# Two stacked graph layers by 2x2 block products: T and V one behind the other in all batches, M2 added by TensorE to a copy of M1 in PSUM, block products in another order

## The chip, the cores and the metric

The kernel runs on one core of a Trainium2 chip. The metric is the device time of one execution in microseconds (us), 2274.87 before (median of 3 runs, 2274.1 to 2276.31). The engines are named as in the profile: PE is TensorE (PEld its weight loads), DVE is VectorE, ACT is ScalarE, POOL is GpSimd, SP issues most DMAs.

## The reference

32 graphs of 512 nodes with 512 features; everything is float32. Two layers, each behind a layer norm and a ReLU, each added to its input:

```python
def _L0_gnn_ref(x, adj, W):
    deg = jnp.sum(adj, axis=-1, keepdims=True)
    agg = jnp.einsum('bij,bjf->bif', adj, x) / jnp.maximum(deg, EPS)
    cat = jnp.concatenate([x, agg], axis=2)
    return jax.nn.relu(jnp.einsum('bnf,of->bno', cat, W))

def _L1_gnn_ref(X, adj, mask, Wqk, Wv):
    q, k = jnp.split(X @ Wqk, 2, axis=-1)
    v = X @ Wv
    agg = jnp.einsum('bij,bjd->bid', adj, k * mask[:, :, None])
    w = inv_scale * mask * jnp.einsum('bid,bid->bi', q, agg)
    return jax.nn.softmax(w, axis=1)[:, :, None] * v

h = jnp.maximum(_layernorm(x, axis=-1), 0.0)
x = x + _L0_gnn_ref(h, adj, L0_gnn_W)
h = jnp.maximum(_layernorm(x, axis=-1), 0.0)
x = x + _L1_gnn_ref(h, adj, nodemask, L1_gnn_Wqk, L1_gnn_Wv)
```

## The kernel before, in words

**What is multiplied.** Per batch there are these products of 512x512 matrices. In layer 0: y = h W2 and o = h W1 + A y, with A the adjacency divided by the degrees. In layer 1, with h1 the normalised second input: u = A (masked h1), T = h1 (Wq Wk^T, scaled) and V = h1 Wv. Since q times the aggregated k is, row by row, the sum of T times u, the scores need only T and u. They are `dot` (T times u summed over a row), `scores`, a maximum over all nodes (`maximum`, on GpSimd), `exponents`, a sum (`row_sum`, on GpSimd) and `weights`. The output is the weights times V (`apply`) plus the layer's input, which a DMA adds (`add_x1`), and `store`.

**Seven block products in place of eight.** Each product is split into 2x2 blocks of 256. Seven products of block sums, M1 to M7, give the four blocks of the result:

- C11 = M1 + M2
- C12 = (M1 + M6) + (M5 + M3)
- C22 = (M1 + M6 + M7) + M5
- C21 = M1 + M6 + M7 + M4

The left operands are the four blocks and three sums of them (seven slots, `left_sums`), the right ones likewise (`right_sums`); the fourth sum overwrites a block. `LEFT` and `RIGHT` say which slot each M uses: M1 and M2 use blocks alone, M5 the first sums (slot 4), M6 the sums in slot 5, M7 those in slot 6. The function `product` does this for y, o and u. The bank `pp` in PSUM collects M1, then M6, M7 and M4 on top, and ScalarE copies the sum out between (`copy`). The bank `pr` holds M2, which VectorE adds to the copy of M1. The bank `pq` collects M5 and M3. One product M is 4 matmuls of 256 columns (8 in o, which has two terms).

**T and V** go one level deeper: each block product is again made of seven, so there are 49 products of 128x128 blocks for T and 49 for V, and the second level's sums (`recombine`, seven VectorE adds a matrix) are made afterwards from the tile `tv`. Both have the same left operand, `h1T`, so `layer1_tv` lays the right operands beside each other and computes T and V together: 49 matmuls of 256 columns, four banks to one M. The function `layer1_one` computes only one of the two, with 128 columns and two banks to one M; the kernel before uses it in its last turn (T and V of batch 30) and for T of batch 31, whose V is a plain `product`.

**Loop and order.** The order of instructions on each engine is written out by hand: `run` steps through a phase (a product M by M, or in half M's), and after each step's matmuls it emits what a `Plan` has at this step; then follows what the product itself does with its bank (a copy or an add). Per turn i of the main loop: o of batch i (14 steps), T and V of batch i-1 (14 steps), u of batch i (7 steps), y of batch i+1 (7 steps). The plans hang onto these steps: loading and normalising x of later batches and turning it by way of DRAM (`FrontH`, whose tile is `n` and whose result is `hT`), the same for the adjacency (`FrontA`: degree sums on ScalarE, `aT`), the second layer norm (`FrontH1`: statistics, `shift` which makes `nmr`, `write` which makes `h1m` and sends it out, `mask`), the block sums, and the tail of the batch before (`Post`). Batch 0 is prepared by `start` (its y and o are computed there), turns 1 and 2 have plans of their own because they also prepare batches 3 and 4, and the last turn has a plan of its own.

[...] The recombination of T is split in the plan: rows 0 in the last steps of T and V, rows 1 in u, each seven adds of 256 columns. The dots follow in u (steps 3 and 4), the scores at step 5, the softmax in y.

## Time and profile before

| What | Before |
|---|---|
| time, median of 3 | 2274.87 us |
| span of the profiled run | 2273.7 us |
| granted TensorE clock | 0.999 |
| DMA, mean over the span | 204 GB/s |
| matmul records on PE | 10526, of which 2940 in T and V together |
| steady period of one batch | 69.50 us |
| T and V in a period: PE, DVE, ACT busy | 21.15, 16.39, 15.03 us |
| last T and V to the end of the span | 68.1 us |

A record of a group has its line, engine, operation, output and inputs by the program's names, shape and count; then the busy time in us and the mean of one in ns; then the idle time just before, and what ended most of it. The names `ptv` and `pw` are the banks of `layer1_tv` and `layer1_one`; `pp_y`, `pq_u`, `pr_o` are those of `product`. Each float32 matmul of the program shows as two records.

### The profile page before, as it was taken

The numbers are of one execution on the slowest core, as the hardware profiler recorded it, in microseconds if no ns is written. First come the engines' busy times: TensorE is split into PE (matmuls) and PEld (weight loads), VectorE is DVE, ScalarE is ACT, GpSimd is POOL, SyncE is SP. The second block draws the span as 40 slices with busy tenths as digits, with TensorE's granted clock in tenths as the row PEclk, the third lists the DMA queues.
The fourth block names the chain that finished last, engine by engine and source line by source line (L and its number), as shares of the span: only waits on it lengthen the run. The fifth ranks groups of instructions, "written<-read, shape, count | busy, mean of one in ns | idle before, by whom it ended". The sixth has DMA issues, their size and how long they took to land.

```text
span 2273.7 us, 32878 instructions
## 1 busy us (share of the span) xinstructions
PE 2249.1 (99%) x10526; PEld 1975.5 (87%) x10526; DVE 1923.7 (85%) x3802; ACT 1026.9 (45%) x1896; POOL 173.2 (8%) x260
## 2 busy tenths in 40 slices
PE   7999999999999999999999999999999999999998
PEld 6788888888888888888888888888888888888897
DVE  6789888888888888888888888888888888888878
ACT  4454444445434554444454344544444543445323
POOL 0000000000010000100000000000000000000000
PEclk9999999999999999999999999999999999999999
DMA  9978787887878787877878778777888787888553
GB/s 220 235 212 244 207 207 190 211 232 204 208 200 202 215 223 203 208 190 209 233 204 207 200 199 218 223 204 208 187 211 230 206 206 200 202 217 218 149 129 90
DMA packets 409772, 463.68 MB, mean 204 GB/s; under 512 B 37728, under 2 KB 271712, under 8 KB 405376
## 3 DMA queue, kind: packets, MB, share of 16 engines
q1 hardware_dynamic: 400192, 428.56, 69.9%
q0 software_dynamic: 8928, 32.51, 8.6%
q8 instruction: 83, 1.36, 0.3%
q14 instruction: 89, 0.73, 0.1%
q10 hardware_dynamic: 480, 0.52, 0.1%
HBM read 293.93 MB, written 167.51 MB: 203 GB/s over the span
## 4 chain that ended last, share of the span: by engine, by line
PE 92%; DMA 3%; DVE 3%; SPq 1%; ACT 1%; issue 0%; POOL 0%; DVEq 0%; POOLq 0%; ACTq 0%
PE ptv L465 28%; PE pp_o L130 18%; PE pp_y L130 9%; PE pq_o L130 9%; PE pp_u L130 9%; PE pr_o L130 5%; PE pq_u L130 5%; PE pq_y L130 5%; PE pr_y L130 2%; PE pr_u L130 2%; PE pw L517 1%; DMA a<-in_adj_dram 1%; DVE tv L94 0%; DMA late<-in_nodemask_dram 0%; SPq L212 0%; DVE mv L97 0%
## 5 line engine op out<-in xcount | busy, mean ns | idle before, releaser
L465 PE MATMUL ptv<-mv,h1T 128*128 128x256 f32 x2940 | 639.7, 379 | 0.1
L465 PEld LDWEIGHTS ptv<-mv,h1T 128*128 128x128 f32 x2940 | 558.5, 190 | 76.4 <-DVE xu L444 0.5
L94 DVE TENSOR_TENSOR tv<-tv 128x256 f32<-128x256 f32 (+1 forms) x658 | 326.9, 509 | 13.5 <-ACT tv L100 1.5
L100 ACT ACTIVATE tv<-ptv 128x512 f32<-128x512 f32 (+1 forms) x360 | 184.9, 541 | 260.0 <-PE ptv L465 259.3
L130 PE MATMUL pp_y<-wide 128*128 128x256 f32 x1024 | 242.6, 380 | 0.9 <-ACT y L100 0.9
L130 PE MATMUL pp_o<-y,aT 128*128 128x256 f32 x1024 | 242.0, 379 | 0.0
L130 PE MATMUL pp_u<-h1m,aT 128*128 128x256 f32 x1024 | 242.0, 379 | 0.0
L130 PE MATMUL pp_o<-w,wide 128*128 128x256 f32 x992 | 234.3, 379 | 0.0
L130 PEld LDWEIGHTS pp_y<-wide 128*128 128x128 f32 x1024 | 194.9, 191 | 27.8 <-ACT y L100 1.3
L130 PEld LDWEIGHTS pp_u<-h1m,aT 128*128 128x128 f32 x1024 | 194.4, 190 | 27.0 <-issue 0.5
L130 PEld LDWEIGHTS pp_o<-y,aT 128*128 128x128 f32 x1024 | 194.4, 190 | 26.7 <-DVE y L97 0.3
L130 PEld LDWEIGHTS pp_o<-w,wide 128*128 128x128 f32 x992 | 188.5, 190 | 25.6
L100 ACT ACTIVATE o<-pp_o 128x512 f32<-128x512 f32 x96 | 57.3, 596 | 294.9 <-PE pp_o L130 294.9
L100 ACT ACTIVATE y<-pp_y 128x512 f32<-128x512 f32 x128 | 76.4, 597 | 235.9 <-PE pp_y L130 235.9
L94 DVE TENSOR_TENSOR tv<-ptv,tv 128x512 f32<-128x512 f32 x240 | 139.7, 614 | 42.9 <-PE ptv L465 39.4
L97 DVE TENSOR_TENSOR h1T<-h1T 128x512 f32<-128x512 f32 (+2 forms) x193 | 165.9, 873 | 1.2
L100 ACT ACTIVATE xu<-pp_u 128x512 f32<-128x512 f32 x128 | 76.4, 597 | 196.1 <-PE pp_u L130 196.1
L246 POOL TENSOR_TENSOR rstd<-rstd,mhalf 128x2 f32<-128x2 f32 (+1 forms) x96 | 78.9, 822 | 651.2 <-DVE rstd L245 651.2
L130 PE MATMUL pq_y<-wide 128*128 128x256 f32 x512 | 121.0, 379 | 0.0
L130 PE MATMUL pq_o<-y,aT 128*128 128x256 f32 x512 | 121.0, 379 | 0.0
L130 PE MATMUL pq_u<-h1m,aT 128*128 128x256 f32 x512 | 120.9, 379 | 0.0
L94 DVE TENSOR_TENSOR tv<-ptv,m_tv 128x512 f32<-128x512 f32 (+1 forms) x120 | 71.9, 622 | 56.4 <-PE ptv L465 54.5
(127 smaller groups left out, 3253.8 us busy)
## 6 DMA issues: line engine op xcount, KB each, us to landing
w<-dw SPq DMA_DIRECT2D x217, 256.0 KB, 4.1
xu<-in_x_dram SPq DMA_DIRECT2D x128, 256.0 KB, 5.4
a<-in_adj_dram SPq DMA_DIRECT2D x256, 128.0 KB, 3.1
dh1T<-h1m SPq DMA_DIRECT2D x128, 256.0 KB, 3.1
dx<-xu SPq DMA_DIRECT2D x32, 1024.0 KB, 4.9
sh1T<-dh1T SPq DMA_DIRECT2D x256, 128.0 KB, 3.2
shT<-dhT SPq DMA_DIRECT2D x248, 128.0 KB, 5.9
daT<-a SPq DMA_DIRECT2D x124, 256.0 KB, 3.0
```

The costliest lines, as they stand in the source:

```text
L94: (on or nc.vector).tensor_tensor(o, a, b, op=ALU.add)
L97: (on or nc.vector).tensor_tensor(o, a, b, op=ALU.subtract)
L100: nc.scalar.activation(o, i, AF.Copy)
L130: nc.tensor.matmul(p[:, rc, :], lt[:, LEFT[k], dk, ts(rc, P)], right[:, dk, :], start=first and n == 0, stop=True, skip_group_check=True,)
L246: nc.gpsimd.tensor_tensor(rstd[:, a:b], rstd[:, a:b], mhalf[:, a:b], op=ALU.pow)
L465: nc.tensor.matmul(banks[n][:, :, ts(i, P)], left[:, LEFT[k], LEFT_IN[j], :], mvR[:, RIGHT[k], RIGHT[j], :, :], start=first and i == 0, st ...
L517: nc.tensor.matmul(banks[n][:, ts(i, P)], held[:, s, :] if held is not None and j == 3 else left[:, s, LEFT_IN[j], :], mvR[:, RIGHT[k], RI ...
```

## The change

Three things. First, `layer1_tv` is gone: in all batches T and then V are computed by `layer1_one`, seven steps' worth of plan in each. This halves the number of banks that one M takes, and V's banks are written only after T's. Second, M2 is no longer put into a bank of its own and added by VectorE. ScalarE copies M1 from its bank into a bank of a new pool `ps_r` (two of the eight banks), and TensorE adds M2 to it there; what is read out is then C11 itself. In y, u, T and V ScalarE copies it out; in o VectorE reads it straight from PSUM. Batch 0's y and o keep the old way (`seed=False`). Third, the order of the block products is M1, M5, M6, M2, M7, M3, M4 in place of M1, M2, M6, M5, M7, M3, M4, so that M2 comes three products after M1. The plans follow: the recombination of T is done in V's steps 1 and 3 with whole rows, the dots and the scores move up in u, and the softmax from y into u.

```diff
-    ps_m = ctx.enter_context(tc.tile_pool(name="ps_m", bufs=8, space=bass.MemoryType.PSUM))
+    ps_m = ctx.enter_context(tc.tile_pool(name="ps_m", bufs=6, space=bass.MemoryType.PSUM))
+    ps_r = ctx.enter_context(tc.tile_pool(name="ps_r", bufs=2, space=bass.MemoryType.PSUM))
...
-    ORDER = [1, 2, 6, 5, 7, 3, 4]
+    ORDER = [1, 5, 6, 2, 7, 3, 4]
...
         pp = mm_tile(f"pp_{name}")
         yield from m(1, pp, True)
-        c11 = place(0, 0)
+        pr = seed_tile(f"pr_{name}")
+        c11 = pr if seed else place(0, 0)
         copy(c11, pp)
-        pr = mm_tile(f"pr_{name}")
-        yield from m(2, pr, True)
-        finish(0, 0, c11, pr, c11)
-        yield from m(6, pp, False)
-        c12 = place(0, 1)
-        copy(c12, pp)
         pq = mm_tile(f"pq_{name}")
         yield from m(5, pq, True)
         m5 = block(f"m5_{name}")
         copy(m5, pq)
+        yield from m(6, pp, False)
+        c12 = place(0, 1)
+        copy(c12, pp)
+        yield from m(2, pr, not seed)
+        if seed:
+            finish(0, 0, None, pr, None)
+        else:
+            finish(0, 0, c11, pr, c11)
         yield from m(7, pp, False)
...
-        yield from parts(1, pp, True, keep(0))
-        yield from parts(2, pr, True, plus(0))
+        yield from parts(1, pp, True, seed)
+        yield from parts(5, pq, True, keep5)
         yield from parts(6, pp, False, keep(1))
-        yield from parts(5, pq, True, keep5)
+        yield from parts(2, pr, False, keep(0))
         yield from parts(7, pp, False, lambda n, p: add(part(3, n), p, m5[n]))
...
-                if not last:
-                    for k in range(7):
-                        p.at(12 + k // 4, post.recombine, k, 0, 0)
-                    run(layer1_tv(i - 1), 14, p)
-                else:
-                    t_plan, v_plan = Plan(), Plan()
-                    for n, fs in p.items():
-                        (t_plan if n < 7 else v_plan)[2 * n % 14] = fs
-                    for k in range(7):
-                        v_plan.at(1 + 2 * (k // 4), post.recombine, k, None, 0)
+                t_plan, v_plan = Plan(), Plan()
+                for n, fs in p.items():
+                    (t_plan if n < 7 else v_plan)[2 * n % 14] = fs
+                for k in range(7):
+                    v_plan.at(1 + 2 * (k // 4), post.recombine, k, None, 0)
+                if last:
                     for c in range(C):
                         v_plan.at(5 + 2 * (c // 2), post.dot, c)
...
-                    run(layer1_one(i - 1, 0), 14, t_plan)
-                    run(layer1_one(i - 1, 1), 14, v_plan)
+                run(layer1_one(i - 1, 0), 14, t_plan)
+                run(layer1_one(i - 1, 1), 14, v_plan)
...
-                for k in range(7):
-                    p.at(1 + k // 4, post.recombine, k, 1, 0)
                 for c in range(C):
-                    p.at(3 + c // 2, post.dot, c)
-                p.at(5, post.scores)
-                p.at(5, post.maximum)
+                    p.at(1 + c // 2, post.dot, c)
+                p.at(2, post.scores)
+                p.at(2, post.maximum)
+                p.at(4, post.shift)
+                p.at(5, post.exponents)
+                p.at(6, post.row_sum)
...
                 if i > 0:
-                    p.at(0, post.shift)
-                    p.at(1, post.exponents)
-                    p.at(2, post.row_sum)
-                    p.at(4, post.weights)
+                    p.at(1, post.weights)
```

More of the change, by code (lines that the diff above doesn't have):

```diff
@@ L91, in mm_tile, with seed_tile @@
         return ps_m.tile([P, 2, H], F32, tag="m", name=name)
+    def seed_tile(name):
+        return ps_r.tile([P, 2, H], F32, tag="r", name=name)
     def add(o, a, b, on=None):
@@ L116, in of, with product @@
         return lambda i: t[:, i]
-    def product(name, terms, place, finish):
+    def product(name, terms, place, finish, seed=True):
         def m(k, p, first):
@@ L432, in layer0_y @@
         y = Y[b] = slots("yh", 1, f"y_{b}")
-        return product(f"y_{b}", [(hT, right(w2R))], *into(y))
+        return product(f"y_{b}", [(hT, right(w2R))], *into(y), seed=b > 0)
     def layer0_out(b, w1):
@@ L444, in finish @@
             nc.vector.scalar_tensor_tensor(dst, p, 0.0, dst, op0=ALU.max, op1=ALU.add)
-        return product(f"o_{b}", [(hT, w1), (AT_[b], right(Y[b]))], place, finish)
+        return product(f"o_{b}", [(hT, w1), (AT_[b], right(Y[b]))], place, finish, seed=b > 0)
     def layer1_u(b):
         return product(f"u_{b}", [(AT_[b], right(H1M[b]))], *into(U[b]))
-    def layer1_tv(b):
-        t = TV[b] = tv
-        left = H1T[b]
-        def m(k, banks, first):
-            for half in ((2, 1), (3, 0)):
-                for n in half:
-                    if first:
-                        banks[n] = mm_tile(f"ptv_{b}_{k}_{n}")
-                    for i, p in enumerate(range(2 * n, min(2 * n + 2, 7))):
-                        j = AT[p]
-                        nc.tensor.matmul(
-                            banks[n][:, :, ts(i, P)],
-                            left[:, LEFT[k], LEFT_IN[j], :],
-                            mvR[:, RIGHT[k], RIGHT[j], :, :],
-                            start=first and i == 0,
-                            stop=True,
-                            skip_group_check=True,
-                        )
-                yield half
-        def part(o, n):
-            first = [0, 4, 8, 10][n] + (2 if n < 2 else 3) * (o % 2)
-            return t[:, o // 2, :, first:first + min(2, 7 - 2 * n), :].rearrange("p w b f -> p w (b f)")
-        def parts(k, banks, first, use):
-            for half in m(k, banks, first):
-                yield
-                for n in half:
-                    use(n, banks[n][:, :, 0:P * min(2, 7 - 2 * n)])
-        def keep(o):
-            return lambda n, p: copy(part(o, n), p)
-        def plus(o):
-            return lambda n, p: add(part(o, n), p, part(o, n))
-        pp, pr, pq, m5 = {}, {}, {}, {}
-        def keep5(n, p):
-            m5[n] = block(f"m5_tv_{b}_{n}")[:, :, 0:P * min(2, 7 - 2 * n)]
-            copy(m5[n], p)
-        yield from parts(1, pp, True, keep(0))
-        yield from parts(2, pr, True, plus(0))
-        yield from parts(6, pp, False, keep(1))
-        yield from parts(5, pq, True, keep5)
-        yield from parts(7, pp, False, lambda n, p: add(part(3, n), p, m5[n]))
-        yield from parts(3, pq, False, plus(1))
-        yield from parts(4, pp, False, keep(2))
     def layer1_one(b, which, held=None):
@@ L549, in layer1_one, with seed @@
         pp, pr, pq, m5 = {}, {}, {}, {}
+        def seed(n, p):
+            pr[n] = seed_tile(f"pr_{which}_{b}_{n}").rearrange("p a f -> p (a f)")
+            copy(like(n, pr[n]), p)
         def keep5(n, p):
@@ L553, in keep5 @@
             copy(m5[n], p)
-        yield from parts(1, pp, True, keep(0))
-        yield from parts(2, pr, True, plus(0))
+        yield from parts(1, pp, True, seed)
+        yield from parts(5, pq, True, keep5)
         yield from parts(6, pp, False, keep(1))
-        yield from parts(5, pq, True, keep5)
+        yield from parts(2, pr, False, keep(0))
         yield from parts(7, pp, False, lambda n, p: add(part(3, n), p, m5[n]))
```

## The prediction

> **What bounds the kernel now.** I read the busy table first, then the chain that ended last (as shares and in order of time), then the groups kept apart by shape, then the timelines of the start, of the first batches and of the end.

> ```profile
> PE 2249.1 (99%) x10526; PEld 1975.5 (87%) x10526; DVE 1923.7 (85%) x3802; ACT 1026.9 (45%) x1896; POOL 173.2 (8%) x260
> ...
> PE 92%; DMA 3%; DVE 3%; SPq 1%; ACT 1%; issue 0%; POOL 0%; DVEq 0%; POOLq 0%; ACTq 0%
> ```

> TensorE is busy 99% of the span and is 92% of the chain. VectorE, which the change relieves, is 85% busy but 3% of the chain. The chain in order of time shows where each batch's time lies (start, duration, what):

> ```profile
> 1232.74 21.15 PE ptv L465 x98
> ...
> 1302.24 21.15 PE ptv L465 x98
> ...
> 1371.74 21.15 PE ptv L465 x98
> ...
> 2205.72 17.97 PE pw L517 x161
> ```

> The period is 69.50 us (1302.24 - 1232.74); 21.15 of it is T and V, 48.35 is u, y and o. TensorE has no gap from 142 us, where T and V of turn 1 end, to 2226 us. So in the steady part only TensorE's own time counts. The fourth line is the key to the change: in its last turn the kernel before already computes T and V one behind the other, with 128-column products.

> ```profile
> L465 PE MATMUL ptv<-mv,h1T 128*128 128x256 f32 x2940 | 639.7, 379 | 0.1
> ...
> L517 PE MATMUL pw<-mv,h1T 128*128 128x128 f32 x280 | 33.9, 277 | 2.2 <-ACT tv L100 1.3 <-DVE tv L94 0.8 <-ACT m_w L100 0.2
> ```

> Each product is two records. The durations (379, 277 ns) overlap; the spacing is what costs: 21.15 us / 98 = 215.8 ns at 256 columns, 17.97 us / 161 = 111.6 ns at 128. Two halves cost 223.2 ns, 7.4 more than the whole.

> [...]

> **The change part by part.**

> *T and V apart.* 49 products of 256 columns become 98 of 128, in 30 turns (2940 records / 98): a batch takes 196 x 111.6 ns = 21.88 us in place of 21.15, so 30 x 0.73 = +21.9 us. All of it is on the path, since TensorE has no gap there.

> *M2 onto a copy of M1.* TensorE's count is unchanged (M2 was computed before). VectorE loses one add in y, u and o (0.69 each) and four at T and V (3 x 0.69 + 0.40), about 4.5 us a batch; ScalarE gains a copy in y and u (0.60 each) and, at T and V, four (2 x 0.60 + 2 x 0.48). ScalarE's new total is about 35 us of 70, so none of this shows in the steady part if no TensorE wait comes of it. A copy into PSUM isn't in the trace: I take the row of a copy out of it (0.60; spacing 0.49 in a run of copies), with 0.45 and 0.9 as bounds.

> *New waits.* A bank of the sum pp is reused two products later. With T and V together a product takes 3.02 us, with one alone 1.56, so the copy out of a bank has about 1.56 + 0.67 us, instead of over 4, before TensorE returns. I walked ScalarE's queue through a normal batch, with spacings from its timeline (h1m write 0.70, mask and degree sum 0.61, copy 0.49 or 0.38). In V: two seeds end at 12.9 us after T starts, mask and degree sum at 14.1, the two M5 copies at 15.0, the next mask at 15.6, the copy of M1+M6 at 16.2; TensorE wants that bank at 10.94 + 6.25 = 17.2. One microsecond is left; in T it is about 1.2. The other new order, M5 second, wants Y's first right sum at the fourth slot of o, 5.2 us in; the trace has it done 2.7 us in. So normal batches: 0.

> *Turn 1* of the loop (its plan also prepares batch 3) doesn't fit:

> ```profile
> 126.48 1.52 ACT L256 ACTIVATE h1m<-xu,nmr,rstd 128x512 f32<-128x512 f32 x2 [2.64 <-DVE nmr L250]
> ...
> 138.11 0.81 ACT L256 ACTIVATE n<-n,nmr,rstd 128x512 f32<-128x512 f32 x1 [3.58 <-DVE nmr L250]
> ```

> ScalarE stands there for VectorE's `nmr`, harmlessly before. After, the write of n (second line) stands in ScalarE's queue ahead of V's copy of M1+M6, and its `nmr` stands in VectorE's queue behind all seven recombinations of T. VectorE, from T's start: 6.1 (statistics of h1, earlier than before by the three adds gone), shift 0.9, transpose 1.2, four statistics 3.2, sums of hT 2.4, adds of M7 and M3 2.2, variance 0.2, seven recombinations 4.9, shift 0.15: 21.2. Then the write 0.70 and the copy 0.6: 22.6. TensorE wants the bank at 17.4: a wait of 5.2 us, with 0.3 more in T where the first line has the same effect. Behind the waiting write are every later copy of V, and M7 and M4 for those. Bounds 2 and 8. Turn 2 is late in the same way, but less (its masks land with a DMA about 15 us in): +0.7, between 0 and 2.

> *Start.* The order in batch 0 is M1, M5, M6, M2; the left and right sums M5 wants are done in time (18.7 of 19.3 us; 34.7 of 36.6). One gap of 1.28 us before M7 of y comes from a VectorE queue that is 0.6 us shorter after: -0.6.

> *End.* From 2217 us on VectorE is nearly the bound:

> ```profile
> 2217.22 2.87 DVE L94 TENSOR_TENSOR tv<-tv 128x512 f32<-128x512 f32 x4 [1.53 <-ACT tv L100]
> ```
> ```profile
> 2226.80 1.83 PE L517 MATMUL pw<-mv,h1T 128*128 128x128 f32 x14 [0.76 <-DVE tv L94]
> ...
> 2249.38 0.94 PE L517 MATMUL pw<-mv,h1T 128*128 128x128 f32 x6 [1.26 <-ACT tv L100]
> ```

> The second fence is TensorE waiting for VectorE's products there. Gone from VectorE's queue are M2's adds of V (0.60 + 0.47, at their spacing), of u (0.60) and of the last T (0.60 + 0.47): 2.7 us, of which nearly all carries through, since the last stage's recombinations, products with u and scores follow one behind the other. The last v's add lay in the wait for the scores' maximum. I take -2.8, between -1 and -4.5.

> *Moved for nothing:* the dots, scores and softmax of the batch move from the end of u and y into u; the maximum comes back in 0.4 us (PARTITION_ALL_REDUCE 381 ns), long before the copy behind the exponential is wanted. The stream of W1 follows the new order with the same loads. The recombinations of T become seven of 512 columns instead of fourteen of 256 (4.9 instead of 5.9 us of VectorE), beside TensorE.

> Sum: 21.9 + 5.2 + 0.3 + 0.7 - 0.6 - 2.8 = +24.7, and 2274.9 + 24.7 = 2299.6 us.

> **The rivals.**
> 1. No bank wait in turns 1 and 2 (a VectorE queue shorter than I walked): 21.9 - 0.6 - 2.8, so 2293.4. For it: VectorE loses work everywhere. Against: the seven recombinations do move ahead of that `nmr`.
> 2. A bank wait in every batch: ScalarE's margin of 1 us is eaten by slower copies into PSUM or late masks. At 0.5 us x 29, 2314; at 1 us, 2329. For it: ScalarE has two more copies in V and half the time for each. Against: the copy would have to take twice its 0.60 us, and ScalarE's busy share in the T and V stretch of a batch is 15.0 of 21.15 us.
> 3. Not slower: VectorE's relief pays and halves cost exactly half, so only start, end and perhaps some jitter change: 2274.9 - 3.4 = 2271.5. Against: the 111.6 ns is measured over 161 records in this very kernel, and TensorE has no gap that a lighter VectorE could close before 2226 us.

> **How the numbers follow.** Forecast 0.60, rival 1 0.20, rival 2 0.15, rival 3 0.05. The time is the forecast's. Below, the range reaches rival 1 with the larger gain at the end (21.9 - 0.6 - 4.5 = +16.8, 2292). Above, it takes the upper bounds of turns 1 and 2 and of the end (21.9 + 8.3 + 2 - 0.6 - 1 = +30.6, 2306) and a first part of rival 2. Left out are most of rival 2 and rival 3, 0.18. Slower by over 0.2% (4.5 us) needs only the +21.9: 0.95, which is all but rival 3. That I split into 0.03 for within 0.2% and 0.02 for faster.

> **What would show it.** Right: 196 records of 128 columns a batch, 21.9 us, period 70.2 us from turn 3 on, TensorE without a gap; one wait of about 5 us for ScalarE in V of turn 1; the end from the last T's start 2.8 us shorter than 68.1 us (2205.6 to 2273.7). Wrong: a spacing near 108 ns, a wait for a ScalarE copy in every period, or a period under 70.

## The result and the profile after

The changed kernel takes 2302.76 us (median of 4 runs, 2300.99 to 2303.08), the kernel before 2274.79 in the same comparison: a ratio of 1.012, interval 1.0103 to 1.0138. It is slower by 28.0 us, where 24.7 was forecast.

The busy table and the chain's shares of the kernel after:

```profile
PE 2272.1 (99%) x13466; PEld 2076.0 (90%) x13466; DVE 1794.3 (78%) x3371; ACT 1120.9 (49%) x2085; POOL 170.1 (7%) x260
...
PE 90%; DVE 4%; DMA 3%; ACT 1%; SPq 1%; issue 1%; POOL 0%; DVEq 0%; POOLq 0%; ACTq 0%
```

VectorE was relieved as meant (1923.7 to 1794.3 us busy), but in the steady part that brought nothing: TensorE is still 99% busy and 90% of the chain, now with 2940 records more. The same kernel's chain in order of time (start, duration, what) in T and V of two successive turns (the 84 records are T's M7, M3 and M4 and V's M1, M5 and M6):

```profile
273.60 9.38 PE pw L475 x84
...
284.55 4.69 PE pw L475 x42
...
343.84 9.38 PE pw L475 x84
...
354.78 4.69 PE pw L475 x42
```

The period is 343.84 - 273.60 = 70.24 us, and a record of 128 columns costs 9.38 / 84 = 111.7 ns. Nothing but TensorE stands in this chain from turn 3 to turn 30.

The two profiled executions, one of each kernel, cut at the same landmarks (the start of T in each turn), give the whole difference of their spans, 2299.11 - 2273.66 = +25.45 us:

| stretch | before | after | difference | forecast |
|---|---|---|---|---|
| up to T of turn 1 | 120.02 | 118.57 | -1.45 | -0.6 |
| turn 1 | 70.08 | 77.12 | +7.03, of which 0.73 records | +5.5 and 0.73 |
| turn 2 | 69.50 | 71.50 | +2.00, of which 0.73 records | +0.7 and 0.73 |
| turns 3 to 30 | 28 x 69.50 | 28 x 70.23 | +20.58 | 28 x 0.73 |
| last T to the end | 68.11 | 65.39 | -2.72 | -2.8 |

Turn 1 holds the one long stop of TensorE. The timelines of TensorE, ScalarE and VectorE there, kernel after (start, duration, engine, instruction, and in brackets the idle time before it and who ended it):

```profile
134.20 1.73 PE L475 MATMUL pr<-mv,h1T 128*128 128x128 f32 x14
140.51 6.99 PE L475 MATMUL pw<-mv,h1T 128*128 128x128 f32 x42 [4.59 <-ACT tv L106]
```
```profile
133.22 0.71 ACT L386 ACTIVATE h1m<-h1m,mraw 128x512 f32<-128x512 f32 x1
139.17 0.81 ACT L265 ACTIVATE n<-n,nmr,rstd 128x512 f32<-128x512 f32 x1 [5.23 <-DVE nmr L259]
139.89 0.95 ACT L106 ACTIVATE tv<-pw 128x512 f32<-128x512 f32 x2
```
```profile
134.19 0.17 DVE L254 TENSOR_SCALAR rstd<-mv 128x4 f32<-128x4 f32 x1
134.27 4.79 DVE L100 TENSOR_TENSOR tv<-tv 128x512 f32<-128x512 f32 x7
138.98 0.15 DVE L259 SCALAR_TENSOR_TENSOR nmr<-mv,rstd 128x4 f32<-128x4 f32 x1
```

Read from below: VectorE does the seven recombinations of T (4.79 us) and only then the small `nmr`. ScalarE, whose next instruction is the write of n that needs `nmr`, stands 5.23 us. Behind it in ScalarE's queue is the copy of V's M1 + M6, and TensorE, which wants to add M7 in the same bank, stands for that copy. The 14 records before take 14 x 0.1117 = 1.56 us and end by the chain's spacing at 135.76, so TensorE loses 140.51 - 135.76 = 4.75 us (the brackets give 4.59, from the modelled end of the last record). Below, the length of a stop is taken from the start of the last record before it to the start of the next, which a trace gives directly; here that is 4.86 us, and one record's 0.11 of it is work.

The stop costs more than itself. Windows of the same kernel around it (us; busy time and count on PE, PEld, DVE, ACT, POOL; then the granted TensorE clock, DMA share, GB/s):

```profile
134.00:137.97 3.97, 1.93 (x18) 1.74 (x16) 3.80 (x8) 0.00 (x0) 1.31 (x1) 1.00 0.00 0
137.97:144.80 6.83, 4.29 (x20) 4.29 (x21) 3.28 (x7) 5.63 (x10) 0.00 (x0) 0.50 0.55 155
144.80:147.30 2.50, 2.50 (x24) 2.50 (x24) 2.46 (x5) 0.66 (x2) 0.00 (x0) 1.00 0.29 94
```

For 6.83 us the granted clock is 0.50 (1.00 is full speed), and TensorE's 20 records in it take 4.29 us, 214 ns each in place of 112: about 2.0 us that the forecast's sum did not have.

### The profile page after: what moved, and what is told of

It is laid out like the page before. It is cut to its first block, busy times and chain, and to the rows that moved or that the text cites. A ratio compares the mean times of both kernels' runs of the same rounds, so it can differ in the third digit from the quotient of the medians.

```text
span 2299.1 us, 38370 instructions
## 1 busy us (share of the span) xinstructions
PE 2272.1 (99%) x13466; PEld 2076.0 (90%) x13466; DVE 1794.3 (78%) x3371; ACT 1120.9 (49%) x2085; POOL 170.1 (7%) x260
## 4 chain that ended last, share of the span: by engine, by line
PE 90%; DVE 4%; DMA 3%; ACT 1%; SPq 1%; issue 1%; POOL 0%; DVEq 0%; POOLq 0%; ACTq 0%
PE pw L475 24%; PE pp_o L136 18%; PE pp_u L136 9%; PE pp_y L136 9%; PE pq_o L136 9%; PE pq_y L136 5%; PE pq_u L136 5%; PE pr_o L136 4%; PE pr L475 4%; PE pr_y L136 2%; PE pr_u L136 2%; DVE tv L100 1%; DMA n<-in_x_dram 1%; DMA a<-in_adj_dram 1%; DVE mv L103 0%
## 5 line engine op out<-in xcount | busy, mean ns | idle before, releaser
L475 PE MATMUL pw<-mv,h1T 128*128 128x128 f32 x5280 | 608.8, 276 | 5.5 <-ACT tv L106 5.5
L475 PEld LDWEIGHTS pw<-mv,h1T 128*128 128x128 f32 x5280 | 602.3, 193 | 8.0 <-ACT tv L106 6.2
L100 DVE TENSOR_TENSOR tv<-tv 128x512 f32<-128x512 f32 (+1 forms) x448 | 299.8, 677 | 9.4 <-ACT tv L106 1.5
L106 ACT ACTIVATE tv<-pw 128x512 f32<-128x512 f32 x252 | 129.9, 543 | 94.3 <-PE pw L475 87.7
L106 ACT ACTIVATE o<-pp_o 128x512 f32<-128x512 f32 x65 | 38.8, 596 | 243.1 <-PE pp_o L136 243.1
L100 DVE TENSOR_TENSOR tv<-pw,m_w 128x512 f32<-128x512 f32 x126 | 77.5, 624 | 87.4 <-PE pw L475 67.9
L106 ACT ACTIVATE pr<-pw 128x512 f32<-128x512 f32 x126 | 66.5, 528 | 158.1 <-PE pw L475 154.3
L106 ACT ACTIVATE y<-pp_y 128x512 f32<-128x512 f32 x97 | 57.8, 596 | 154.1 <-PE pp_y L136 154.1
L106 ACT ACTIVATE xu<-pp_u 128x512 f32<-128x512 f32 x96 | 57.3, 597 | 137.3 <-PE pp_u L136 137.3
```

Source lines behind the costliest of these rows:

```text
L100: (on or nc.vector).tensor_tensor(o, a, b, op=ALU.add)
L106: nc.scalar.activation(o, i, AF.Copy)
L475: nc.tensor.matmul(banks[n][:, ts(i, P)], held[:, s, :] if held is not None and j == 3 else left[:, s, LEFT_IN[j], :], mvR[:, RIGHT[k], RI ...
```

## The experiments

Theory A, the forecast's: the time is TensorE's records (+0.73 us in each of 30 turns) plus queue waits in turns 1 and 2, less what is gained at the start and the end; M2's new way is worth nothing where TensorE has no gap. Rival B: the steady 0.73 us is a cost of the new order, of the seeding or of bank reuse rather than of the record count. Rival C: the wait in turn 1 is something other than the order of ScalarE's and VectorE's queues.

**1. The records alone.** The kernel before, with only the matmul of `layer1_tv` halved in place; order, banks, adds and plans are as before:

```diff
-                        nc.tensor.matmul(
-                            banks[n][:, :, ts(i, P)],
+                        for w in range(2):
+                            nc.tensor.matmul(
+                                banks[n][:, w, ts(i, P)],
...
-                                start=first and i == 0,
+                                start=first and i == 0 and w == 0,
```

> The kernel before, with each 256-column matmul of T and V split in place into two of 128 columns (T's, then V's half with the same weights); order, banks, copies, plans of before. Theory (the loss per turn is a price of each record, whatever the order): period 70.23 us, no wait that before hasn't, 2274.9 + 31 x 0.73 = 2297. Rival (128 columns are dear only where the weights change or banks are few): period near 69.5, 2275.

Measured: 2297.14 us against 2275.3, a ratio of 1.0095 (1.0079 to 1.0112). Its chain in order of time, T and V of two turns:

```profile
331.07 21.88 PE ptv L466 x196
...
401.31 21.88 PE ptv L466 x196
```

The stretch is 21.88 us, what 196 x 111.6 ns gave, and the period 401.31 - 331.07 = 70.24. The count of records alone makes the steady cost; rival B falls. The forecast of no new wait missed by a little: turn 2 takes 70.73 us, 0.50 more than the later turns.

**2. T and V apart, everything else as before** (M2 by VectorE, old order; only the recombination of T moves into V, as in the kernel after):

```diff
-                if not last:
-                    for k in range(7):
-                        p.at(12 + k // 4, post.recombine, k, 0, 0)
-                    run(layer1_tv(i - 1), 14, p)
-                else:
...
+                run(layer1_one(i - 1, 0), 14, t_plan)
+                run(layer1_one(i - 1, 1), 14, v_plan)
```

> The kernel before with T and V one behind the other in all turns, M2 still added by VectorE, order and pools of before. Theory: 196 records of 128 columns a turn, period 70.23 us from turn 3 on (+22 us in all), and a wait in turn 1 at least as long as in the changed kernel (VectorE has more to do): 2302 to 2308. Rival (the loss comes with M1's copies or the order): below 2280.

Measured: 2307.64 us against 2274.91, a ratio of 1.0142 (1.0128 to 1.0156). Its periods are 80.76 (turn 1), 72.06 (turn 2), then 70.23, and its end takes 68.06. Set beside the kernel after, this shows what the rest of the change (seeds, order and moved plans together) is worth: nothing in turns 3 to 30 (70.23 in both), 3.6 us in turn 1 (80.76 - 77.12), where VectorE's queue is what the others wait for, and 2.7 us at the end (68.06 - 65.39). Without it TensorE stops for 6.02 us in V of turn 1 and for 1.66 us in T. No run has the seeds without the new order, so how the two share in this is not shown.

**3. The rest of the change, with T and V together:** the new order and the seeds stay in y, o, u and in the last turn; all other turns have `layer1_tv` again, its M2 added by VectorE, with two of its banks taken from the seeds' pool, and the recombinations, dots and softmax stand in u and y as before. The edit is shown against the kernel after.

```diff
+                if not last:
+                    for k in range(7):
+                        p.at(12 + k // 4, post.recombine, k, 0, 0)
+                    run(layer1_tv(i - 1), 14, p)
+                else:
...
+                    run(layer1_one(i - 1, 0), 14, t_plan)
+                    run(layer1_one(i - 1, 1), 14, v_plan)
```

> The changed kernel with T and V together again in all turns but the last (256-column products, M2 of T and V added by VectorE there), and the plan of u and y as before; y, u, o and the last turn keep the M1 copy in PSUM and the new order. Theory (the whole loss is the 128-column products and turns 1 and 2): period 69.50 us in every turn from 3 on, the start 1.4 us and the end 2.7 us shorter than before: 2270.7. Rival (copies into PSUM, the new order or the smaller bank pools cost something in every turn): above 2275.

Measured: 2272.98 us (13 runs) against 2274.91, a ratio of 0.9993 (0.9984 to 1.0001). The period is back at 69.50 us, and the end takes 65.35, so the end's gain needs neither T and V apart in the other turns nor the moved plans; but turn 1 takes 71.24 us, 1.2 more than before. TensorE's timeline and VectorE's, at the border of turns 1 and 2:

```profile
167.66 1.89 PE L136 MATMUL pq_o<-w,wide 128*128 128x256 f32 x8
171.03 1.99 PE L136 MATMUL pq_o<-y,aT 128*128 128x256 f32 x8 [1.48 <-DVE y L103]
```
```profile
161.72 1.25 DVE L287 STREAM_TRANSPOSE aT<-saT 128x1024 f32<-128x1024 f32 x1 [1.58 <-DMA saT<-daT]
...
165.83 1.41 DVE L100 TENSOR_TENSOR tv<-tv 128x512 f32<-128x512 f32 x2
...
167.76 1.41 DVE L100 TENSOR_TENSOR tv<-tv 128x512 f32<-128x512 f32 x2
...
169.69 0.68 DVE L100 TENSOR_TENSOR tv<-tv 128x512 f32<-128x512 f32 x1
170.29 1.41 DVE L103 TENSOR_TENSOR y<-y 128x512 f32<-128x512 f32 x2
```

M5 in second place wants Y's right sum (the last line), which stands in VectorE's queue behind seven recombinations of V (the last five are in the three `tv` lines shown); and the queue is late because it had waited for the transposed adjacency (first line). This is a price of the new order, which wants that sum earlier. The prediction had compared the two only for normal batches and put the price there at nothing; in turn 1 of this kernel it is a stop of 1.86 us (169.17 to 171.03). The same kernel again:

> The same kernel as e2_tv_together, for comparison on the same chip: 2273.0.

Measured: 2272.71 us (21 runs) against 2274.86, a ratio of 0.999 (0.9983 to 0.9996), with a stop of 1.71 us that ends at 171.42.

**4. That wait taken away:** four of the seven recombinations are done behind Y's right sums instead, in turn 1 alone.

```diff
                 p.at(0, right_y[2])
+                if i == 2:
+                    for k in range(3, 7):
+                        p.at(0, post.recombine, k, None, 1)
...
-                    for k in range(7):
+                    for k in range(3 if i == 1 else 7):
                         p.at(3 + k // 2, post.recombine, k, None, 1)
```

> The kernel of e2_tv_together with four of V's seven recombinations moved, in turn 1 only, from y of batch 2 to the start of o of batch 2, behind Y's first two right sums. Theory (the one gap of 1.86 us that e2's trace has in its loop is M5's second term waiting for Y's first right sum, which M5 wants four stages earlier in the new order): the gap goes, 1.7 us less than e2 in the same call, 2271.3. Rival (the aT transposes, which land late there, hold that sum up whatever stands before it): no change against e2.

Measured: 2270.68 us (17 runs, 2269.86 to 2272.04) against 2274.86, a ratio of 0.9981 (0.9974 to 0.9989). Turn 1 takes 69.50 us like all others, and TensorE has no idle entry between 127 and 300 us. That is 2.0 us less than with the wait (2272.71), and faster than both kernels: by 4.2 us than before, by 32.1 than after. In the profiled executions the gain over the kernel before is 2.7 us at the end, 0.6 in turn 1 and the rest in the start, which varies.

**5. The queue order of turn 1.** Three versions of the kernel after. The first moves the seven recombinations of T in turn 1 to later steps of V, the second moves the writes of n to later steps, the third does both.

```diff
-                    v_plan.at(1 + 2 * (k // 4), post.recombine, k, None, 0)
+                    v_plan.at((9 if i == 1 else 1) + 2 * (k // 4), post.recombine, k, None, 0)
```
```diff
-                        p.at(9 + c, fh.write, c)
+                        p.at([10, 10, 11, 12][c], fh.write, c)
```

> The changed kernel with only the recombinations of T moved later in V of turn 1. Theory: nmr comes 3.5 us earlier, TensorE still waits about 1.2 us for the copy of M1+M6; a gap so short leaves the clock alone: turn 1 about 71.6 us, time 2297.3. Rival (clock drops with any wait there): turn 1 about 73.5 us, 2299.2.

> The changed kernel with only the writes of n moved behind the copy of M1+M6 in turn 1; the recombinations of T stay ahead of VectorE's add of M7. Theory: the wait moves from the copy to that add, 1.5 us before M4, no half clock: turn 1 about 71.9 us, time 2297.6. Rival (clock drops with any wait there): about 2 us more.

> The changed kernel with turn 1 alone re-ordered: the seven recombinations of T two stages later in V, and the writes of n behind the copy of M1+M6. Theory (the wait in V of turn 1 is the write of n standing behind nmr, and its 4.9 us gap halves the TensorE clock for 6.8 us): turn 1's period falls from 77.1 to about 70.3 us, no half-clock stretch there, time 6.9 us less, 2295.9. Rival (the half clock has another cause): the gap goes but a half-clock stretch of some 6 us stays, 4.9 us less, 2297.9.

| version | us (4 runs each) | ratio to before, interval | turn 1 | turn 2 |
|---|---|---|---|---|
| after | 2302.76 | 1.012 (1.0103 to 1.0138) | 77.12 | 71.50 |
| recombinations later | 2297.38 | 1.0099 (1.0086 to 1.0113) | 72.78 | 71.96 |
| writes later | 2295.62 | 1.0089 (1.0072 to 1.0106) | 72.25 | 70.62 |
| both later | 2295.72 | 1.009 (1.0076 to 1.0104) | 72.08 | 72.22 |

Each of the three takes 4.3 to 5.0 us out of turn 1, and in none does the granted clock fall there: behind the stops in V the 8 records of one block product of u still take 1.73 us, as in the steady turns. Rival C falls: the wait is the order of the two queues. The forecasts of the sizes were less good than two of the times make them look. Turn 1 came out longer than expected in all three (72.78, 72.25 and 72.08 for 71.6, 71.9 and 70.3), so that 2297.38 for 2297.3 and 2295.72 for 2295.9 are partly luck, and the 2 us by which the version with the writes later beat its forecast don't come from turn 1. None reaches 70.23, for each leaves smaller waits. With the writes later one of them is the wait of experiment 3, M5 for Y's right sum, 1.42 us long: the long stop had hidden it. With both later, TensorE and VectorE:

```profile
140.82 0.94 PE L475 MATMUL pw<-mv,h1T 128*128 128x128 f32 x6 [0.97 <-DVE tv L100]
```
```profile
137.44 2.86 DVE L100 TENSOR_TENSOR tv<-tv 128x512 f32<-128x512 f32 x4
140.22 0.55 DVE L100 TENSOR_TENSOR tv<-pw,m_w 128x384 f32<-128x384 f32 x1
```

The moved recombinations now stand ahead of the add that reads M7's second bank, and M4 waits for that bank. Turn 1 has more VectorE work than places for it.

**6. What a stop of TensorE costs beyond its length.** The kernel after, with 7, 11, 15, 19, 23 or 27 small copies of unused data (extra work) on ScalarE ahead of V's copy of M1 + M6, in turns 4 to 27, so each length comes four times:

```diff
+    scr = const.tile([P, 64], F32, name="scr")
+    nc.vector.memset(scr, 1.0)
...
+                if 4 <= i < 28:
+                    for k in range([7, 11, 15, 19, 23, 27][(i - 4) % 6]):
+                        v_plan.at(4, copy, scr, scr)
```

> The changed kernel with work added: in V of turns 4 to 27, ahead of the copy of M1+M6, 7, 11, 15, 19, 23 or 27 small ScalarE copies (64 columns, on a scratch tile, not used), so that TensorE gets gaps of about 1 to 6 us, each length in four turns. Theory (an idle TensorE loses half its clock): gaps under some 2 us are followed by records at 111.7 ns, gaps of 4 us and more by a stretch of several us at 213 ns, in nearly every turn with such a gap. Rival (turn 1's slow stretch had another cause): 111.7 ns after every gap.

Measured (one execution, 2437.98 us): the length of each stop, what it added to its period of 70.23, and how long the granted clock was at half:

| stop, us | added to the period, us | clock at half, us |
|---|---|---|
| 1.28 (x4) | 1.27 | none |
| 2.65, then 2.43 (x3) | 2.64, then 4.05 | none, then 3.41 |
| 3.58 (x4) | 5.05 to 5.20 | 3.41 |
| 4.73 (x4) | 7.19, 6.08, 7.55, 6.14 | 6.83, 3.41, 6.83, 3.41 |
| 5.88 (x4) | 7.73 to 8.50 | 6.83 |
| 7.03 (x4) | 8.59 to 8.99 | 6.83 |

Windows of two of the stops (columns as above), the stretch before the clock falls and the stretch at half:

```profile
501.12:504.53 3.41, 0.39 (x4) 0.20 (x2) 0.84 (x2) 3.08 (x12) 0.00 (x0) 1.00 1.05 305
504.53:507.94 3.41, 3.13 (x14) 3.13 (x15) 0.69 (x1) 3.30 (x8) 0.00 (x0) 0.50 0.06 23
572.80:579.62 6.82, 3.99 (x36) 3.80 (x34) 4.30 (x9) 6.35 (x22) 0.00 (x0) 1.00 1.09 263
579.62:586.45 6.83, 5.21 (x24) 5.21 (x25) 2.43 (x4) 4.55 (x12) 0.00 (x0) 0.50 0.02 6
```

The first stop ends at 504.81, 0.28 us after its slow block has begun: in the 3.41 us before, with TensorE busy for 0.39, the clock is still at 1.00, and TensorE pays while it is already working again. The stops of 4.73 us, about the length in the kernel after, cost 1.35 to 2.8 us on top of themselves.

Up to turn 3 this program has the instructions of the kernel after, and so shows how much their waits vary: turn 1 takes 78.12 us here and turn 2 72.95 (77.12 and 71.50 in the other execution), and T of turn 3 starts 2.35 us later.

## Why the prediction was right, step by step

- *T and V apart, +21.9.* Right. 0.735 us in each of 28 steady turns, and the experiment with the halved records alone gives +21.8 in all (2297.14 - 2275.3). The spacing read from the last turn of the kernel before was good for every turn.
- *M2 on a copy of M1: nothing in the steady part.* Right, shown by experiments 2 and 3: the period is 70.23 us with the seeds (the kernel after) and without (experiment 2), and 69.50 with them in y, u and o (experiment 3) as before. The copy into PSUM takes a mean of 582 ns at 128x512, where 0.60 was assumed: among the groups by shape of the kernel after,

```profile
L106 ACT ACTIVATE tv<-pr 128x512 f32<-128x512 f32 x63 | 37.8, 600 | 0.0
L106 ACT ACTIVATE m_w<-pw 128x512 f32<-128x512 f32 x63 | 37.2, 590 | 12.9 <-PE pw L475 12.9
L106 ACT ACTIVATE pr<-pw 128x512 f32<-128x512 f32 x63 | 36.7, 582 | 154.3 <-PE pw L475 154.3
```

  the last line writes PSUM, the first two write SBUF, all three read PSUM: PSUM as destination is some 8 to 18 ns shorter here, too little to matter.
- *A wait for a bank in V of turn 1, 5.2 us.* Right in place, cause and size of the stop (4.75): the walk through the queues has TensorE back 22.6 us after T's start, the trace 21.9 (140.51 - 118.57). Mis-sized by what follows it: the half clock adds about 2.0 us, which no term of the sum held. The 0.3 us in T did not come in this execution, and the kernel before's own small waits in turn 1 went away (70.08 us is 0.58 above its later turns). So turn 1 cost 6.3 where 5.5 was forecast.
- *Turn 2, 0.7.* Mis-sized: 1.27, most of it in two stops of TensorE (0.70 and 0.44 us long) for ScalarE's copies. That is inside the bounds given; in experiment 6 the same instructions took 2.72 us over the steady period, outside them.
- *Normal batches, 0 (rival 2).* Right: the microsecond of slack held in 28 turns. The other slack, M5 second against Y's right sum, held as well in the kernel after. In turn 1 it did not hold in experiment 3 (a stop of 1.86 us) nor with the writes later in experiment 5 (1.42), so there the kernel after owes it to its longer stop.
- *Start, -0.6.* The profiled pair shows -1.45, but this stretch varies from one execution to the next: with the old start T of turn 1 begins at 118.68, 119.49 and 120.02 us in three profiles (mean 119.40), with the new one at 117.86 to 119.42 in eight (mean 118.54). The difference of the means, -0.86, fits. The gap before M7 of y that was to go is there in all three old profiles and gone or down to 0.17 us in the new ones.
- *End, -2.8.* Right in size (-2.72) and in place. The chain that ended last leaves T and V 18.1 us after the last T's start in the kernel before and 17.1 us in the kernel after (at 2223.69 and 2250.80), and from there it is mostly VectorE's, for 50.0 and 48.3 us. TensorE's stops shrink by about the same amount. From the start of the last T to batch 31's V TensorE takes 48.25 us in the kernel before and 45.46 after; records alone would take 44.91 (T and V 21.88, u 12.09, T of batch 31 10.94), so 3.34 us of stops became 0.55. The kernel before's wait of 1.26 us in T of batch 31 answers to this line of TensorE's timeline, kernel after:

```profile
2275.28 1.16 PE L475 MATMUL pw<-mv,h1T 128*128 128x128 f32 x8 [0.28 <-ACT tv L106]
```

- *Rivals.* 1 (no wait in turns 1 and 2) falls with the timelines; 2 with the period; 3 with experiment 1.

The sum of the terms as measured is +25.45 for the profiled execution, which is the fastest of the four. That it lies so near to +24.7 is partly luck: turns 1 and 2 cost 1.4 us more than forecast, and the start gave 0.85 more. The other three executions took 1.7 to 2.1 us more than this one. The waits of turns 1 and 2, which differ by 2.45 us between two executions of the same instructions (this one and experiment 6), are enough for that, and the start varies too; these three have no trace, so it stays open which it was.

## What to carry to other kernels

Where TensorE has no gap, count its records and multiply by the spacing that the chain shows: relief of another engine is then worth only what it gives at the start, at the end and in irregular turns (here VectorE's busy time fell by 129.4 us, and the steady period rose by the records' 0.73 us all the same). Look for new waits in the turns whose plan is not the usual one, and there follow each engine's queue by hand: a tiny instruction (here `nmr`, 0.15 us) behind long ones can stop two other engines. Where one wait is taken away, look for the next one that it had hidden. A change of three parts can hide a gain in one of them; here the new order with the seeds of y, u and o, and one wait removed, is 4.2 us faster than before, and the halved products alone cost 22 us.

## What the runs showed of the hardware

```profile
429.44:432.85 3.41, 1.84 (x16) 1.84 (x17) 0.59 (x1) 3.24 (x9) 0.00 (x0) 1.00 0.85 291
1794.77:1798.18 3.41, 1.40 (x12) 1.41 (x13) 0.46 (x2) 3.25 (x11) 0.00 (x0) 1.00 0.97 309
1490.98:1494.39 3.41, 2.55 (x12) 2.55 (x13) 0.38 (x1) 3.38 (x10) 0.00 (x0) 0.50 0.00 0
1037.01:1040.42 3.41, 2.88 (x13) 2.88 (x14) 0.69 (x1) 3.41 (x8) 0.00 (x0) 0.50 0.03 5
```

The 2.65 us stop lay across two windows and left 1.84 us busy in the emptier one (first line): the clock stayed. The 2.43 us stop of turn 23 lay almost wholly in one window and left 1.40 (second line): the next window ran at half. At half clock, 2.55 us busy was followed by a second window at half (third line, turn 19, 6.83 us in all), and 2.88 by the full clock (fourth line, turn 13, 3.41 us in all). The kernel after, cut in the same way around its stop:

```profile
134.55:137.97 3.42, 1.38 (x13) 1.19 (x11) 3.28 (x6) 0.00 (x0) 1.27 (x1) 1.00 0.00 0
137.97:141.38 3.41, 0.86 (x4) 0.87 (x5) 1.76 (x4) 2.21 (x5) 0.00 (x0) 0.50 0.16 59
141.38:144.80 3.42, 3.42 (x18) 3.42 (x18) 1.51 (x3) 3.42 (x7) 0.00 (x0) 0.50 0.94 250
144.80:148.21 3.41, 3.41 (x29) 3.31 (x29) 3.37 (x7) 1.31 (x3) 0.00 (x0) 1.00 0.41 129
```

1.38 us busy was followed by half clock, 0.86 at half by half again, and 3.42 by the full clock. Where between these figures the outcome changes was not measured. Stops of equal length cost differently in experiment 6 (those of 4.73 us added 6.08 to 7.55); that this comes from where a stop falls in such windows is an estimate from these lines, not shown by a run of its own.

Accumulating by TensorE onto what ScalarE has put into PSUM costs TensorE no time that the runs show: with seeds in y, u and o (experiment 4) and without (the kernel before) the period is 69.50 us, and with T and V apart it is 70.23 us with seeds everywhere (the kernel after) and without (experiment 2).
